# Comparing the tiles of a block with one another for eight pairs of blocks at a time

## The chip, the cores and the metric

The kernel runs on one core of a Trainium2 chip. The metric is the device time of one execution in microseconds (us), and a kernel's time is the median of its runs. The engines are named as in the profile: PE (matrix multiplications), PEld (its weight loads), DVE (vector), ACT (activations), POOL (GpSimd) and SP (which issues DMAs here).

## What is computed

The reference is one residual layer of a graph network, with 12,500 nodes of 64 numbers and 212,500 edges, sorted by `dst`:

```python
def _L0_gnn_ref(h, row, col, dist, eW1, eb1, eW2, eb2, nW1, nb1, nW2, nb2):
    edge_in = jnp.concatenate([h[row], h[col], dist], axis=1)
    e = jax.nn.silu(edge_in @ eW1 + eb1)
    e = jax.nn.silu(e @ eW2 + eb2)
    agg = jax.ops.segment_sum(e, row, num_segments=h.shape[0])
    node_in = jnp.concatenate([h, agg], axis=1)
    out = jax.nn.silu(node_in @ nW1 + nb1) @ nW2 + nb2
    return out
h = jnp.maximum(_layernorm(x, axis=-1), 0.0)
x = x + _L0_gnn_ref(h, src, dst, edge_weight1, ...)
```

The sum runs over `row`, which is `src`: the edges come in the order of the other end, so they have to be brought together by `src` first.

## The kernel before

The nodes are dealt into NB = 100 buckets of 125 by their number modulo 100, and an edge belongs to the bucket of its `src`. The kernel is a counting sort through HBM, followed by dense work on each bucket.

*Blocks and pairs.* The edges are taken in 208 blocks of 1024 (`BLK`), and a block is TB = 8 tiles of 128 edges, one edge on each partition. Two blocks are a pair, and there are NP = 104 pairs. Three tiles in SBUF hold, for every edge, its bucket (`bkE`), its node in the bucket (`locE`) and the first row of its bucket in the HBM table `q` (`offE`). Each is [128 partitions, 16 tiles of a pair, 104 pairs], so the pair is the innermost index, and two tiles of one pair lie 104 numbers (416 bytes) apart. `sources` and `scale` fill them: for pairs 0 to 3 (FIRST = 4) first, and for pairs 4 to 103 in one go later.

*Counting a block: `count(s)`, on DVE and PE.* It is a generator in three parts.
- First part: `oh` (L354) compares the buckets of the block's 8 tiles with the 100 bucket numbers, `each` (L362) sums that over the tiles, and `pick` (L364, or L366 for a whole pair) makes the one-hot columns for the gather of target rows.
- Second part: two small matmuls (L371, L389) carry the running counts `full` in PSUM over from block to block and over the 128 partitions. Then, for the first block of a pair, four DVE instructions (L396 to L402) work for both blocks of the pair. They find, for each edge, how many of the earlier tiles of its block have an edge of the same bucket on the same partition, and add that to `offE`: `eq` compares the 8 tiles with one another, is multiplied by `early` (1 for an earlier tile, times G = 4), is summed into `pre`, and `pre` is added to `offE`.
- Third part: `mine` (L404) and `rank` (L406) read the running count of each edge's bucket, and `to` (L408) adds it to `offE`. That is the edge's row in `q`. `to` has four buffers.

*Sending a block: `send(s)`.* PE gathers the target side of each edge (L429), ACT copies it to `qs` (L439) with the node's number behind it (L445), and POOL writes each tile of 128 edges to the rows `to` of `q` by an indirect DMA (L452): eight to a block, 1661 in all. `qs` has eight buffers of four tiles each. `send(s)` and `count(s + 1)` go hand in hand, part by part.

*The groups.* As ranks fill up, level by level (`LEVELS`), the rows of a bucket are loaded back from `q`, four buckets at a time, and the 450 steps of edge work run over them: `s_lr`, `s_one_t` (`oneT`, L533), `s_pt` (L542, L548), `s_one` (`one`, L561), `s_p2` (L580), `s_seg` (L594), `s_add` (L603, L605). At the end the node network runs bucket group by bucket group (`nodes`).

*The order.* PE, DVE, ACT and SP follow the order in which the program is written. In the first 150 us or so the parts of `send` and `count` alternate with the preparation of the node tables (`norm`, `products` and so on, through `feed`). Later they stand between the steps of the groups, at places that `marks` computes from the levels. POOL has little besides its indirect DMAs. `cnt` is a pool with one buffer for each name, `wk` one with two.

Of the kernel before, what the change touches and what calls it, by code (L numbers as in the profile page):

```python
# [28 lines left out]
F32 = mybir.dt.float32  # L29
# [4 lines left out]
OP = mybir.AluOpType  # L34
AX = mybir.AxisListType
# [3 lines left out]
P = 128  # L39
# [9 lines left out]
TB = BLK // P  # L49
# [12 lines left out]
FIRST = 4  # L62
# [11 lines left out]
def tile_gnn(ctx: ExitStack, tc: tile.TileContext, x, src, dst, ew, eW1, eb1, eW2, eb2, nW1, nb1, nW2, nb2, out):  # L74
    nc = tc.nc
# [6 lines left out]
    NP = -(-E // PAIR)  # L82
# [101 lines left out]
    early = const.tile([P, TB, TB], F32, name="early")  # L184
# [25 lines left out]
    bkE = const.tile([P, 2 * TB, NP], F32, name="bkE")  # L210
    locE = const.tile([P, 2 * TB, NP], F32, name="locE")
    offE = const.tile([P, 2 * TB, NP], F32, name="offE")
# [52 lines left out]
    wk = ctx.enter_context(tc.tile_pool(name="wk", bufs=2))  # L265
    cnt = ctx.enter_context(tc.tile_pool(name="cnt", bufs=1))
    qsp = ctx.enter_context(tc.tile_pool(name="qs", bufs=8))
    top = ctx.enter_context(tc.tile_pool(name="to", bufs=4))
    with ExitStack() as work:
# [59 lines left out]
        def weights(s):  # L329

            if s < nblocks:
                p, g = s // 2, s % 2
                pick = lists[p][1][:, g]
                e0 = s * BLK
                m = 1 if p == 0 or e0 + 2 * BLK > E else 2
                if m == 2 or e0 + BLK <= E:
                    of = bass.AP(tensor=ew.tensor, offset=ew.offset + e0, ap=[[QR, NQR], [BLK, m], [1, QR]])
                    nc.sync.dma_start(lists[p][1][WL::32, g : g + m, :], of)
                else:
                    for a in range(NQR):  # L340
                        m = min(QR, E - e0 - a * QR)
                        if m > 0:
                            of = bass.AP(tensor=ew.tensor, offset=ew.offset + e0 + a * QR, ap=[[m, 1], [1, m]])
                            nc.sync.dma_start(pick[a * 32 + WL : a * 32 + WL + 1, :m], of)

        def count(s):

            if s < nblocks:
                bc, win, pick = blk[s]
                p, g = s // 2, s % 2  # L350
                whole = p > 0 and (2 * p + 2) * BLK <= E
                buckets = bkE[:, g * TB : (g + 1) * TB, p]
                oh = wk.tile([P, TB, NB], BF16, name="oh")
                nc.vector.tensor_tensor(  # L354
                    oh,
                    numbers[:, None, :].to_broadcast([P, TB, NB]),
                    buckets[:, :, None].to_broadcast([P, TB, NB]),
                    op=OP.is_equal,
                )
                each = wk.tile([P, NB], BF16, name="each")  # L360
                with nc.allow_low_precision("whole numbers up to eight"):
                    nc.vector.tensor_reduce(each, oh.rearrange("p t b -> p b t"), AX.X, OP.add)  # L362
                if not whole:
                    nc.vector.tensor_scalar(pick, bc, same, plus, op0=OP.is_equal, op1=OP.add)  # L364
                elif g == 0:
                    nc.vector.tensor_scalar(lists[p][1], lists[p][0], same, plus, op0=OP.is_equal, op1=OP.add)  # L366
            yield
            if s < nblocks and (g == 0 or not whole):
                weights(s)
            if s > 0:  # L370
                nc.tensor.matmul(full, rest, sums.pop(), start=False, stop=True, skip_group_check=True)  # L371
            limits = [(SURE[w], OP.is_gt) for w in ready_at if s == ready_at[w]]
            closed = s > 0 and (s == nblocks or needed[s] != needed[s - 1])
            if closed:
                limits.append((SURE[needed[s - 1]], OP.is_lt))
            if s == nblocks:
                limits.append((ROWS, OP.is_gt))
            if limits:
                u = wk.tile([P, NB], F32, name="u")
                v = wk.tile([P, 1], F32, name="v")  # L380
            for limit, op in limits:
                nc.vector.tensor_scalar(u, full, float(G * limit - 1), None, op0=op)
                nc.vector.tensor_reduce(v, u, AX.X, OP.max)
                nc.vector.tensor_tensor(bad[:, 1:2], bad[:, 1:2], v, op=OP.add)
            if s == nblocks:
                return
            if closed and LEVELS[needed[s - 1]][2]:
                nc.vector.tensor_scalar(full, full, float(G * ENDS[needed[s - 1]] - 1), None, op0=OP.max)
            nc.tensor.matmul(full, before, each, start=False, stop=True, skip_group_check=True)  # L389
            sums.append(each)  # L390
            if g == 0:
                assert p in scaled
                both = bkE[:, :, p].rearrange("p (g t) -> p g t", g=2)
                wide = [P, 2, TB, TB]
                eq = wk.tile(wide, F32, name="eq")
                nc.vector.tensor_tensor(  # L396
                    eq, both[:, :, :, None].to_broadcast(wide), both[:, :, None, :].to_broadcast(wide), op=OP.is_equal
                )
                nc.vector.tensor_tensor(eq, eq, early[:, None].to_broadcast(wide), op=OP.mult)
                pre = wk.tile([P, 2 * TB], F32, name="pre")  # L400
                nc.vector.tensor_reduce(pre.rearrange("p (g t) -> p g t", g=2), eq, AX.X, OP.add)
                nc.vector.tensor_tensor(offE[:, :, p], offE[:, :, p], pre, op=OP.add)  # L402
            yield
            nc.vector.tensor_tensor(mine, oh, full[:, None, :].to_broadcast([P, TB, NB]), op=OP.mult)  # L404
            rank = wk.tile([P, TB], F32, name="rank")
            nc.vector.tensor_reduce(rank, mine, AX.X, OP.add)  # L406
            to = top.tile([P, TB], I32, name="to")
            nc.vector.scalar_tensor_tensor(  # L408
                to, rank, float(G * ROWS - 1), offE[:, g * TB : (g + 1) * TB, p], op0=OP.min, op1=OP.add
            )  # L410
            blk[s].append(to)
            yield
# [60 lines left out]
        def send_all(s0, s1):  # L473

            for s in range(s0, s1):
                load(s + 2)
                i, rest = divmod(s - FILL0, FILL_EACH)
                if rest == 0 and 0 <= i < len(fills):
                    fill(*fills[i])

                for j, _ in enumerate(itertools.zip_longest(send(s), count(s + 1))):
                    pending[needed[s]] -= j == PIECES - 1
                    yield
# [319 lines left out]
        done_a, done_b, ready, scaled = [], [], set(), set()  # L803
# [9 lines left out]
        with tc.tile_pool(name="lists", bufs=1, side="right") as lp:  # L813
# [40 lines left out]
            list(scale(0, FIRST))  # L854
            load(0)
            counting = count(0)
            next(counting)
            todo = groups()
# [47 lines left out]
        for k in range(first, len(steps) + 2):  # L906
            for s in turn:
# [17 lines left out]
                else:  # L925
                    f, ahead = s
# [146 lines left out]
```

## Time and profile before

| | us |
|---|---|
| median of 3 runs | 2463.26 (2462.79 to 2467.51) |
| the profiled execution | 2461.7 |
| its span, first to last instruction | 2459.9 |
| busy: PE | 2045.2 (83%) |
| busy: DVE | 1936.9 (79%) |
| busy: POOL | 1705.5 (69%) |
| busy: ACT | 1088.8 (44%) |
| DVE's four instructions L396 to L402 | 121.7 |

Times in the profile are us from the start of the span. "Busy" is time in which an engine executes an instruction. A wait is put down to whatever released it last. The page has the busy shares in 40 slices of the span, the chain of work that ended last (followed back from the last instruction) and the groups of instructions by cost. The timeline lists single instructions with start and length, and in brackets how long the engine had been idle and what ended that.

### The profile page before, as it was taken

To read this page: it belongs to the slowest core of one execution; us is meant where nothing else is said; L and a number is where in the kernel's file an instruction comes from. 1 tells how busy PE (TensorE), PEld (TensorE's weight loads), DVE (VectorE), ACT (ScalarE), POOL (GpSimd) and SP (SyncE) were. 2 spreads that over 40 slices of the span, in tenths; PEclk is the share of its full clock that TensorE was granted. 3 is DMA by queue.
4 is the path that set the end of the run, shared out by engine and by line. 5 is a ranking of instruction groups with operands and counts; after the bars stand their busy time and mean duration, and the time that the engine had idled before them with its cause. 6 is when DMAs were issued, how large, how long until landed. Compare 5 with 4: busy or idle time off the path is not lost.

```text
span 2459.9 us, 46292 instructions
## 1 busy us (share of the span) xinstructions
PE 2045.2 (83%) x16191; PEld 1829.8 (74%) x16191; DVE 1936.9 (79%) x3006; ACT 1088.8 (44%) x2403; POOL 1705.5 (69%) x1712
## 2 busy tenths in 40 slices
PE   3673776665688898898998988899999999999997
PEld 2452665555587787787887877888888898999986
DVE  7895777676787898787888788898889899886432
ACT  2452333222344454454544444454555555554442
POOL 4777777777777777777777777777777777762110
PEclk9575898877899999999999998999999999999999
DMA  4563566555666765667654544455555556665652
GB/s 116 185 217 124 168 186 193 183 175 171 210 212 211 219 210 180 215 215 227 194 166 165 166 156 161 154 182 165 177 172 181 179 166 207 215 199 174 193 162 67
DMA packets 237006, 443.85 MB, mean 180 GB/s; under 512 B 49804, under 2 KB 108735, under 8 KB 236561
## 3 DMA queue, kind: packets, MB, share of 16 engines
q1 hardware_dynamic: 158629, 269.79, 35.9%
q0 software_dynamic: 53536, 123.03, 14.3%
q10 hardware_dynamic: 24602, 47.98, 6.7%
q8 instruction: 132, 2.16, 0.4%
q14 instruction: 107, 0.88, 0.1%
HBM read 251.07 MB, written 189.55 MB: 179 GB/s over the span
## 4 chain that ended last, share of the span: by engine, by line
PE 36%; DMA 17%; DVE 16%; POOL 13%; issue 8%; ACT 2%; DVEq 0%; POOLq 0%; ACTq 0%; SPq 0%
DMA q<-qs,to 16%; POOL q L452 13%; PE seg L594 8%; PE pt L548 8%; PE p L580 7%; PE pt L542 4%; PE qp L429 4%; DVE oh L354 2%; DVE each L362 2%; DVE oneT L533 2%; PE lr L528 2%; DVE aggT L605 2%; DVE one L561 2%; DVE mine L404 1%; DVE rank L406 1%
## 5 line engine op out<-in xcount | busy, mean ns | idle before, releaser
L452 POOL DMA_INDIRECT q<-qs,to x1661 | 1676.4, 1009 | 586.3 <-issue 396.9
L552 ACT ACTIVATE e<-pt 128x512 f32<-128x512 f32 x450 | 268.7, 597 | 849.8 <-PE pt L548 839.2
L594 PE MATMUL seg<-one,e 128*128 128x125 f32 x3600 | 504.0, 285 | 110.2 <-DVE aggT L605 77.7
L594 PEld LDWEIGHTS seg<-one,e 128*128 128x128 f32 x3600 | 456.0, 199 | 140.0 <-issue 84.7
L580 PEld LDWEIGHTS p<-w,e 128*128 128x128 f32 x3600 | 472.3, 197 | 37.4 <-issue 17.8
L548 PE MATMUL pt<-oneT,a 125*128 125x128 f32 (+1 forms) x2400 | 487.1, 338 | 15.3 <-DVE oneT L533 15.3
L580 PE MATMUL p<-w,e 128*128 128x128 f32 x3600 | 494.1, 281 | 0.0
L548 PEld LDWEIGHTS pt<-oneT,a 125*128 125x128 f32 x2400 | 366.9, 200 | 35.4 <-DVE oneT L533 18.2
L439 ACT COPY qs<-qp 128x512 f32<-128x512 f32 x416 | 224.9, 588 | 356.8 <-PE qp L429 310.1
L533 DVE TENSOR_SCALAR oneT<-lr,part 125x512 f32<-125x512 f32 x450 | 335.0, 745 | 43.4 <-PE lr L528 42.8
L362 DVE TENSOR_REDUCE each<-oh 128x100 bf16<-128x800 bf16 x208 | 315.9, 1519 | 7.2
L561 DVE TENSOR_TENSOR one<-nodes,qt 128x500 f32<-128x500 f32 x450 | 302.4, 672 | 0.2 <-issue 0.2
L542 PE MATMUL pt<-ident,qt 128*128 128x128 f32 x1800 | 287.6, 285 | 1.3 <-DVE oneT L533 1.3
L429 PE MATMUL qp<-win,pick 64*128 64x256 f32 x1662 | 266.3, 435 | 24.2 <-DMA pick<-in_edge_weight_dram 9.1
L584 ACT ACTIVATE e<-p 128x512 f32<-128x512 f32 x450 | 268.7, 597 | 28.7 <-PE p L580 28.7
L574 ACT COPY p<-b2f 128x512 f32<-128x512 f32 x450 | 267.2, 594 | 0.0
L605 DVE TENSOR_TENSOR aggT<-aggT,seg 128x500 f32<-128x500 f32 x275 | 184.0, 669 | 65.5 <-PE seg L594 62.7
L408 DVE SCALAR_TENSOR_TENSOR to<-rank,offE 128x8 int32<-128x8 f32 x208 | 36.2, 174 | 251.3 <-DMA q<-qs,to 246.5
L429 PEld LDWEIGHTS qp<-win,pick 64*128 64x128 f32 x1662 | 162.5, 203 | 81.1 <-issue 44.3
L542 PEld LDWEIGHTS pt<-ident,qt 128*128 128x128 f32 x1800 | 200.7, 148 | 21.3 <-issue 13.4
L406 DVE TENSOR_REDUCE rank<-mine 128x8 f32<-128x800 f32 x208 | 205.1, 986 | 7.2
L404 DVE TENSOR_TENSOR mine<-oh,counts 128x800 f32<-128x800 bf16 x208 | 203.9, 980 | 8.3 <-PE counts L389 8.0
(145 smaller groups left out, 1454.3 us busy)
## 6 DMA issues: line engine op xcount, KB each, us to landing
qt<-q SPq DMA_DIRECT2D x150, 576.0 KB
a<-ta SPq DMA_DIRECT2D x300, 256.0 KB
qt<-q SPq DMA_DIRECT2D x150, 288.0 KB
q<-zeros ACTq DMA_DIRECT2D x25, 1080.0 KB
q<-qs,to POOLq DMA_INDIRECT x1661
q<-zeros ACTq DMA_DIRECT2D x10, 1440.0 KB
bc<-dests SPq DMA_DIRECT2D x103, 128.0 KB
win<-tb SPq DMA_DIRECT2D x416, 30.0 KB
```

Source lines behind the costliest of these rows:

```text
L362: nc.vector.tensor_reduce(each, oh.rearrange("p t b -> p b t"), AX.X, OP.add)
L429: nc.tensor.matmul(qps[i][:, t, : n_of[t]], pick[at, t * P : (t + 1) * P], win[at, : n_of[t]], start=True, stop=True)
L452: ins = nc.gpsimd.indirect_dma_start(out=q[:], out_offset=bass.IndirectOffsetOnAxis(ap=to[:k, j : j + 1], axis=0), in_=qs[:k, t, a, :], in ...
L533: nc.vector.tensor_scalar(oneT, st[k].pop("lr")[:L], part1[:L, :], None, op0=OP.is_equal)
L542: nc.tensor.matmul(pt[:, t, :], qt[:, j, :H], ident, is_transpose=True, start=t == 0, stop=False, skip_group_check=True)
L548: nc.tensor.matmul(pt[:, cols, :], a[:L, b, :], oneT[:, cols, :], start=False, stop=True, skip_group_check=True)
L552: nc.scalar.activation(e1, pt, AF.Silu)
L561: nc.vector.tensor_tensor(one.rearrange("p (b j) l -> p b j l", j=n), nodes1[:, None, None, :].to_broadcast(wide), loc[:, tiles[0][1] : ti ...
L574: nc.scalar.copy(p2, b2f)
L580: nc.tensor.matmul(p2[:, t, :], e1[:, t, :], w2, start=False, stop=t == G - 1, skip_group_check=True)
L584: nc.scalar.activation(e2, p2, AF.Silu)
L594: nc.tensor.matmul(item[2][:, b, :], e2[:, t, :], one[:, t, :], start=j < G, stop=j >= G * (n - 1))
```

## The change

In place of four DVE instructions for each pair, a new function `earlier(g, p0, p1)` does the same for one of the two blocks (`g`) of the pairs `p0` to `p1`, with the pair innermost in `eq` and `pre`. It is called for one pair at a time for pairs 0 to 3, and for eight at a time (EACH) after that: at pair 2 for the first blocks of pairs 4 to 11, at pair 3 for their second blocks, at pairs 10 and 11 for pairs 12 to 19, and so on. The last calls, at pairs 98 and 99, are for the four pairs 100 to 103. So there are 8 calls of one pair, 24 of eight and 2 of four, with four instructions each. `eq` moves from the pool `wk` to `cnt`. The instructions of the other engines and their order stay.

```diff
+        EACH = 8
+
+        def earlier(g, p0, p1):
+
+            if p0 >= p1:
+                return
+            n = p1 - p0
+            wide = [P, TB, TB, n]
+            of = bkE[:, g * TB : (g + 1) * TB, p0:p1]
+            eq = cnt.tile([P, TB, TB, EACH], F32, name="eq")[:, :, :, :n]
+            nc.vector.tensor_tensor(
+                eq, of[:, :, None, :].to_broadcast(wide), of[:, None, :, :].to_broadcast(wide), op=OP.is_equal
+            )
+            nc.vector.tensor_tensor(eq, eq, early[:, :, :, None].to_broadcast(wide), op=OP.mult)
+            pre = wk.tile([P, TB, EACH], F32, name="pre")[:, :, :n]
+            nc.vector.tensor_reduce(pre, eq.rearrange("p t u n -> p t n u"), AX.X, OP.add)
+            off = offE[:, g * TB : (g + 1) * TB, p0:p1]
+            nc.vector.tensor_tensor(off, off, pre, op=OP.add)
+
         def count(s):
...
             if g == 0:
                 assert p in scaled
-                both = bkE[:, :, p].rearrange("p (g t) -> p g t", g=2)
-                wide = [P, 2, TB, TB]
-                eq = wk.tile(wide, F32, name="eq")
-                nc.vector.tensor_tensor(
-                    eq, both[:, :, :, None].to_broadcast(wide), both[:, :, None, :].to_broadcast(wide), op=OP.is_equal
-                )
-                nc.vector.tensor_tensor(eq, eq, early[:, None].to_broadcast(wide), op=OP.mult)
-                pre = wk.tile([P, 2 * TB], F32, name="pre")
-                nc.vector.tensor_reduce(pre.rearrange("p (g t) -> p g t", g=2), eq, AX.X, OP.add)
-                nc.vector.tensor_tensor(offE[:, :, p], offE[:, :, p], pre, op=OP.add)
+                if p < FIRST:
+                    earlier(0, p, p + 1)
+                    earlier(1, p, p + 1)
+                ahead = (p - FIRST) % EACH - (EACH - 2)
+                if ahead >= 0:
+                    p0 = p + 2 - ahead
+                    assert all(i in scaled for i in range(p0, min(p0 + EACH, NP)))
+                    earlier(ahead, p0, min(p0 + EACH, NP))
```

## The prediction

> **What bounds the kernel now.** I read the groups by cost first, then one line over stages, then the chain and the waits, then the timeline.
>
> The first view, the page's costliest groups, gives the scatter on POOL (L452: one indirect DMA per 128 edges) and DVE's last step ahead of it (L408, which writes the offsets `to`). The columns are busy us and mean ns, then idle us before it and what ended most of it. The second view is L452 alone in stages: length, busy us, count.
>
> ```profile
> L452 POOL DMA_INDIRECT q<-qs,to x1661 | 1676.4, 1009 | 586.3 <-issue 396.9
> L408 DVE SCALAR_TENSOR_TENSOR to<-rank,offE 128x8 int32<-128x8 f32 x208 | 36.2, 174 | 251.3 <-DMA q<-qs,to 246.5
> 200.00:2065.00 1865.00, 1430.19 (x1424) 0.93 0.58 183
> ```
>
> 1430.19/1424 is 1.004 us of work for each scatter; the timeline shows 0.30 to 0.31 us between two. 1424 x (1.004 + 0.305) = 1864 us of a stage of 1865 us: from 200 to 2065 us POOL is full. DVE is 79% busy over the span, but it waits 246.5 us at L408 for scatters to finish, because `to` has four buffers. So DVE is ahead, and POOL sets the pace. The chain's last link of that kind over 3 us is at 2068 us:
>
> ```profile
> 1926.08 4.21 DMA q<-qs,to
> 2068.53 3.17 DMA q<-qs,to
> ```
>
> After it PE is the bound (97 to 98% busy from 2100 to 2300 us), and POOL waits for the last blocks.
>
> What lengthens a scatter? The median is 967 ns, the mean 1009: 1661 x 0.042 = 70 us in all. The timeline shows whom it meets (start us, length us):
>
> ```profile
> 1385.95 0.67 DVE L561 TENSOR_TENSOR one<-nodes,qt 128x500 f32<-128x500 f32 x1
> 1386.04 1.42 POOL L452 DMA_INDIRECT q<-qs,to  x1 [0.30 <-issue]
> 1000.88 0.39 DVE L396 TENSOR_TENSOR eq<-bkE 128x128 f32<-128x128 f32 x1
> 1001.07 1.06 POOL L452 DMA_INDIRECT q<-qs,to  x1 [0.31 <-issue]
> 1018.07 1.50 DVE L362 TENSOR_REDUCE each<-oh 128x100 bf16<-128x800 bf16 x1
> 1018.28 0.96 POOL L452 DMA_INDIRECT q<-qs,to  x1 [0.30 <-issue]
> ```
>
> A scatter that starts inside a tensor_tensor with both inputs in SBUF ends 0.84 us after it (1386.62 to 1387.46). The reduce does nothing to it. So an instruction of length T costs POOL (T - 0.15)^2 / (2 x 1.27) us on average: the scatter must start in its first T - 0.15 us, out of a period of 1.27. For L561 that is 0.106 us, x450 = 48 us of the 70.
>
> **The change, part by part.** Prices of the four steps come from the groups with shapes kept apart:
>
> ```profile
> L396 DVE TENSOR_TENSOR eq<-bkE 128x128 f32<-128x128 f32 x104 | 41.6, 400 | 0.0
> L399 DVE TENSOR_TENSOR eq<-eq,early 128x128 f32<-128x128 f32 x104 | 30.4, 292 | 3.6
> L401 DVE TENSOR_REDUCE pre<-eq 128x16 f32<-128x128 f32 x104 | 29.8, 286 | 3.5
> L402 DVE TENSOR_TENSOR offE<-offE,pre 128x16 f32<-128x16 f32 x104 | 19.9, 191 | 3.6
> L406 DVE TENSOR_REDUCE rank<-mine 128x8 f32<-128x800 f32 x208 | 205.1, 986 | 7.2
> L362 DVE TENSOR_REDUCE each<-oh 128x100 bf16<-128x800 bf16 x208 | 315.9, 1519 | 7.2
> L754 DVE SCALAR_TENSOR_TENSOR bkE<-locE,srcE 128x64 f32<-128x64 f32 x1 | 0.2, 224 | 0.0
> ```
>
> *Removed:* 104 x 1.169 = 121.7 us of DVE.
> *Added:* a base of 0.157 us and 1.04 ns an element fit L399, L406 and L754. L396 reads every element 416 bytes apart and pays 1.90 ns; L362 reads 200 bytes apart and pays 1.70. With pairs innermost, eight lie together: I price comparison and product of 512 elements as L754, which has four together (0.157 + 0.533 = 0.690 us each; other end 1.13 at L396's rate). The reduce steps 32 bytes: L362's rate, 1.03 us (ends 0.69 and 1.13). The addition of 64: 0.224. A full call is 2.63 us, and there are 24; two calls of four pairs at 1.63; eight calls of one pair (64 elements) at about 0.97. That is 63.2 + 3.3 + 7.8 = 74 us, so DVE is relieved of 47 us. From 200 to 2065 us this is worth nothing in itself: the cover is the wait at L408, which should grow by about that. Instructions and waits of the other engines, DMAs included, keep their order in the built program. A burst of 2.6 us in place of 1.2, in two of eight pairs, stands ahead of `mine`, `rank` and `to` on DVE; PE and ACT wait for those behind it, and POOL has 17 to 28 us of ready `qs` in that stage. If that cover were gone, each burst would cost 1.4 us.
>
> *The start.* There the cover is thin, and pairs 0 to 3 still run alone, each as two calls, while pairs 2 and 3 run a full call as well. Pitches: two single calls take 1.93 us on DVE where the old group took 1.18, so +0.75; with a full call (2.65) 4.58, so +3.4.
>
> ```profile
> 79.61 0.40 DVE L396 TENSOR_TENSOR eq<-bkE 128x128 f32<-128x128 f32 x1
> 80.98 0.95 DVE L631 TENSOR_REDUCE var<-xs 128x12 f32<-128x768 f32 x1
> 90.19 0.26 ACT L445 COPY qs<-locE 128x64 f32<-128x64 f32 x1
> 93.05 0.97 POOL L452 DMA_INDIRECT q<-qs,to  x1 [0.30 <-ACT rows_a L207]
> 110.65 0.25 ACT L445 COPY qs<-locE 128x64 f32<-128x64 f32 x1
> 114.38 0.96 POOL L452 DMA_INDIRECT q<-qs,to  x1 [0.31 <-issue]
> ```
>
> DVE works without a break to 80 us, and POOL idles 6 us before 82.88, so pair 0's 0.75 shifts everything; pair 1's is swallowed by the 1.03 us that L404 waited at 46.82 for PE. Pair 2's stands ahead of `var` at 80.98, for which ACT waits, with PE's transposes and block 4's `qs` behind it: 79.61 + 4.58 is 84.2, 3.2 later, of which 0.1 was slack. Pair 3's adds 3.4, so DVE is 0.75 + 3.1 + 3.4 = 7.25 us late when block 6's `qs` is made. That `qs` was ready at 110.90, and POOL took it at 114.38, 3.48 later; 0.28 is the least lag seen. So POOL slips by 7.25 - 3.20 = 4.0 us, and, being full afterwards, never makes it up. At contiguous rates throughout it is 2.8, at L396's rate for all 6.5.
>
> *POOL's lengthening.* Before: 49 of the 104 `eq` follow L561 directly in the timeline, overlapping by 0.09 us, so the two act as one hold of 0.98 us: 49 x (0.271 - 0.106) = 8.1, the other 55 x 0.025 = 1.4, the products 0.8; 10.3 us. After: 10 of 24 full calls follow L561: hold 1.27, 10 x (0.494 - 0.106) = 3.9; 14 x 0.115 = 1.6; the products, 24 x 0.115 = 2.8; 8.3 us. So -2.0. The ends: -10.3 if long instructions met no scatter, +6.3 with `eq` at 1.13 us. Chance of the phases alone, over 450 L561 with a spread of 0.16 us each, is +-3.4 us.
>
> The Trainium skill (SBUF — State Buffer, "Who interferes with whom") speaks both ways here. It says the shared port is held for a whole instruction, which is against fewer, longer ones; but it infers that tensor_tensor does not stall descriptor generation, and the 1.06 and 1.42 us scatters above say it does. By that inference this part would be 0 and the sum +3.5.
>
> *The tail.* Past 2065 us DVE loses some 5 groups, with PE at 97%: PE waited 1.2 us there for DVE's L605, so -0.5.
>
> **Sum:** 4.0 - 2.0 - 0.5 = +1.5 on the profiled execution's 2461.7 us (span 2459.9 and 1.8 around it), 2463.2. It lies 1.6 below the median of the runs, 2463.26; on that median the forecast is 2465 us: no change that can be told, 0.2% or 4.9 us being about what a measurement can.
>
> **Rivals.**
> *DVE is the bound after all, and its 47 us come off.* For: 79% busy, 16% of the chain. Against: the 246.5 us of L408, and POOL full to 1 us in 1865. All of it gives 2416; by DVE's share of the chain, 0.16 x 47 = 7.5, it is 2456. 0.10, nearly all near the second.
> *The port is held longer.* On DVE's comparison, in 24 places: from about 0.9 us an `eq` (in place of 0.69) the scatters' lengthening is 11.8, +1.5 on before, and with the start's 4.0 and tail it passes 4.9; at 1.13 us the sum is 6.3 + 4.0 - 0.5, 2473. For: L396's own slow rate. Against: L754. 0.20.
> *The start costs more.* If single calls and full calls run at L396's rate, 6.5 - 2.0 - 0.5 gives 2467; unfavourable phases carry it past 4.9. 0.18.
> *The fused calls don't relieve DVE* (the reduce is as slow as what it replaces): the time stays in the forecast's range, since DVE has room, and its chance is in the forecast's.
>
> **How the numbers follow.** The forecast has 0.50; 0.38 goes to slower (0.20 and 0.18) and 0.12 to faster (DVE's 0.10 and 0.02 of lucky phases). The range of 2457 to 2474 takes the start's 2.8 to 6.5, phases of +-4.4 (1.28 x 3.4), the slow `eq`, and DVE's share nearly to its end; the forecast's own is 2459 to 2468.
>
> **What would show it.** DVE's four lines sum to about 74 us in place of 122; the full `eq` at 0.69 and the full reduce at 1.03; the wait at L408 near 290 us; the mean scatter within 5 ns of 1009; POOL's 49th scatter about 4 us later than 114.38, and full from then to 2065. I am wrong if POOL shows gaps in the middle, if the mean scatter moves by 5 ns or more, or if L408's wait shrinks.

## The result, and the profile after

| | before | after |
|---|---|---|
| median, us | 2463.07 (18 runs, 2459.42 to 2469.38) | 2469.08 (18 runs, 2462.81 to 2474.86) |
| ratio to before | | 1.002, interval 1.001 to 1.0029 |
| the profiled execution, us | 2461.7 | 2474.24 |

The changed kernel is about 6 us slower. The profiled execution of it is among the slowest of its 18, so the 12.5 us between the two profiles are not the size of the change; the profile is read for places.

The costliest groups of the changed kernel (busy us, mean ns, idle us before, what ended most of it), and its scatter in the stage from 200 to 2065 us:

```profile
L469 POOL DMA_INDIRECT q<-qs,to x1661 | 1680.5, 1012 | 595.3 <-issue 397.9
L425 DVE SCALAR_TENSOR_TENSOR to<-rank,offE 128x8 int32<-128x8 f32 x208 | 36.1, 173 | 278.1 <-DMA q<-qs,to 274.1
200.00:2065.00 1865.00, 1429.12 (x1417) 0.93 0.58 183
```

The scatter is L469 now and the step that writes the offsets L425. POOL is nearly as full as before: 1417 x (1.0085 + 0.305) is 1861 of 1865 us. DVE waits 274.1 us for scatters in place of 246.5. That is 28 of the 46 us that it was relieved of; its waits for PE grew as well (75.4 us for 62.7 ahead of `aggT`, 54.7 for 42.8 ahead of `oneT`).

DVE's groups of the changed kernel, with shapes kept apart: comparison, product, sum and addition in the calls of eight pairs, then two of them in the calls of one.

```profile
L356 DVE TENSOR_TENSOR eq<-bkE 128x512 f32<-128x512 f32 x24 | 16.4, 684 | 0.0
L359 DVE TENSOR_TENSOR eq<-eq,early 128x512 f32<-128x512 f32 x24 | 16.6, 693 | 0.8
L361 DVE TENSOR_REDUCE pre<-eq 128x64 f32<-128x512 f32 x24 | 26.0, 1082 | 0.8
L363 DVE TENSOR_TENSOR offE<-offE,pre 128x64 f32<-128x64 f32 x24 | 5.6, 233 | 0.8
L356 DVE TENSOR_TENSOR eq<-bkE 128x64 f32<-128x64 f32 x8 | 2.2, 276 | 0.0
L361 DVE TENSOR_REDUCE pre<-eq 128x8 f32<-128x64 f32 x8 | 2.2, 269 | 0.3
```

The prices are those foreseen. A full call is 2.69 us, and all calls together are 76 us in place of 122. So the 6 us were not lost on DVE's own account.

The timeline shows where POOL falls behind: at the start. In the changed kernel, ACT's copies that complete the first `qs` of blocks 4 and 6, and POOL's 33rd and 49th scatters, which take them up:

```profile
95.41 0.26 ACT L462 COPY qs<-locE 128x64 f32<-128x64 f32 x1
95.94 0.97 POOL L469 DMA_INDIRECT q<-qs,to  x1 [1.76 <-ACT hr L664]
119.40 0.25 ACT L462 COPY qs<-locE 128x64 f32<-128x64 f32 x1
119.92 0.96 POOL L469 DMA_INDIRECT q<-qs,to  x1 [3.27 <-ACT qs L462]
```

Before, these two scatters started at 93.05 and 114.38 us without a wait. Now POOL waits 1.76 and 3.27 us for rows to send, and its 49th scatter is 5.5 us late. From there POOL is nearly full in both kernels. Up to the 1501st scatter it stands still for 5.4 us beyond the 0.304 us between two scatters, before for 2.2; most of that is four gaps of 0.58 to 2.21 us, where before had one of 1.16 us. The longest:

```profile
884.71 1.28 POOL L469 DMA_INDIRECT q<-qs,to  x1 [2.21 <-issue]
```

At the 1501st scatter the changed kernel's profile is 13.8 us behind (2030.2 and 2016.4): 5.5 us from the start, 3.2 from these gaps, and 5.1 from scatters that lasted longer.

### The profile page after: what moved, and what is told of

Same layout as the page of the kernel before. It is cut to its first block, busy times and chain, and to the rows that moved or that the text cites. A ratio compares the mean times of both kernels' runs of the same rounds, so it can differ in the third digit from the quotient of the medians.

```text
span 2472.5 us, 46004 instructions
## 1 busy us (share of the span) xinstructions
PE 2050.6 (83%) x16191; PEld 1834.2 (74%) x16191; DVE 1899.8 (77%) x2726; ACT 1088.4 (44%) x2403; POOL 1709.5 (69%) x1712
## 4 chain that ended last, share of the span: by engine, by line
PE 39%; DMA 18%; DVE 14%; POOL 13%; issue 8%; ACT 2%; DVEq 0%; POOLq 0%; ACTq 0%; SPq 0%
DMA q<-qs,to 17%; POOL q L469 13%; PE seg L611 9%; PE pt L565 8%; PE p L597 8%; PE pt L559 4%; PE qp L446 4%; PE lr L545 2%; DVE oneT L550 2%; DVE oh L373 2%; DVE each L381 2%; DVE one L578 2%; DVE aggT L622 1%; DVE mine L421 1%; DVE rank L423 1%
## 5 line engine op out<-in xcount | busy, mean ns | idle before, releaser
L469 POOL DMA_INDIRECT q<-qs,to x1661 | 1680.5, 1012 | 595.3 <-issue 397.9
L550 DVE TENSOR_SCALAR oneT<-lr,part 125x512 f32<-125x512 f32 x450 | 335.0, 744 | 55.1 <-PE lr L545 54.7
L425 DVE SCALAR_TENSOR_TENSOR to<-rank,offE 128x8 int32<-128x8 f32 x208 | 36.1, 173 | 278.1 <-DMA q<-qs,to 274.1
L622 DVE TENSOR_TENSOR aggT<-aggT,seg 128x500 f32<-128x500 f32 x275 | 184.0, 669 | 77.1 <-PE seg L611 75.4
L446 PEld LDWEIGHTS qp<-win,pick 64*128 64x128 f32 x1662 | 164.0, 205 | 83.2 <-issue 41.9
```

What stands on the lines that cost most here:

```text
L446: nc.tensor.matmul(qps[i][:, t, : n_of[t]], pick[at, t * P : (t + 1) * P], win[at, : n_of[t]], start=True, stop=True)
L469: ins = nc.gpsimd.indirect_dma_start(out=q[:], out_offset=bass.IndirectOffsetOnAxis(ap=to[:k, j : j + 1], axis=0), in_=qs[:k, t, a, :], in ...
L550: nc.vector.tensor_scalar(oneT, st[k].pop("lr")[:L], part1[:L, :], None, op0=OP.is_equal)
```

## The experiments

The theory of the start says that the loss is made in the first 120 us, where POOL has under 4 us of ready rows, and is never made up. The rivals: longer comparisons hold POOL's scatters up (the port), and DVE's relief is worth something in the middle. All ratios are to the kernel before, run beside them.

**One half, then the other.** The calls of eight begin with pair 12, and pairs 0 to 11 keep the old group:

```diff
+                if p < FIRST + EACH:
+                    both = bkE[:, :, p].rearrange("p (g t) -> p g t", g=2)
...
-                if p < FIRST:
-                    earlier(0, p, p + 1)
-                    earlier(1, p, p + 1)
                 ahead = (p - FIRST) % EACH - (EACH - 2)
-                if ahead >= 0:
+                if p >= FIRST and ahead >= 0:
```

> Pairs 0 to 11 keep the old group of four instructions for each pair; calls of eight pairs begin with pairs 12 to 19. So the first 130 us are those of before, and the middle is that of the changed kernel. Theory of the start (the loss is made where POOL has under 4 us of ready rows): the 49th scatter starts at 114.4 us as before, and the time is before's within 2 us, 2461 to 2465. Rival, the port (long comparisons hold POOL's scatters up): the loss stays, +4 to +7, with a mean scatter over 1.012 us. Rival, DVE's relief is worth something in the middle: under 2460.

Measured: 2464.51 us (12 runs), ratio 1.001, interval 0.9999 to 1.002. POOL's 49th scatter, and all its scatters:

```profile
114.41 0.97 POOL L477 DMA_INDIRECT q<-qs,to  x1 [0.30 <-issue]
L477 POOL DMA_INDIRECT q<-qs,to x1661 | 1683.7, 1014 | 588.6 <-issue 393.0
```

The start is that of before, and most of the loss is gone. DVE's relief in the middle brought nothing. Whether 2 us of loss or none are left, this run does not say. The mean scatter is 1.014 us, over the 1.012 that the port rival named, but the loss that it named is not there; further down this length turns out to be that of `one`, not of the comparisons.

The other half: single calls for pairs 0 to 3 and one call for each half of pairs 4 to 11, then the old group.

```diff
                 if p < FIRST:
                     earlier(0, p, p + 1)
                     earlier(1, p, p + 1)
+                if p >= FIRST + EACH:
+                    both = bkE[:, :, p].rearrange("p (g t) -> p g t", g=2)
...
-                if ahead >= 0:
+                if p < FIRST and ahead >= 0:
```

> The other half: single calls for pairs 0 to 3 and one call of eight for each half of pairs 4 to 11, then the old group for each pair from 12 on. Theory of the start: the whole loss is here, 49th scatter near 119.9 us, time +4.5 to +6.5 on before. The port: 49th scatter as late, but made up or not seen at the end, time within 2 us of before.

Measured: 2468.28 us (12 runs), ratio 1.0027, interval 1.0016 to 1.0038.

```profile
119.60 0.97 POOL L480 DMA_INDIRECT q<-qs,to  x1 [3.27 <-ACT qs L473]
```

The whole loss is here, in twelve pairs of 104, with the same wait of 3.27 us. The theory of the start holds.

**A smaller burden on the start.** The changed kernel, but with the old group for pairs 0 to 3:

```diff
                 if p < FIRST:
-                    earlier(0, p, p + 1)
-                    earlier(1, p, p + 1)
+                    both = bkE[:, :, p].rearrange("p (g t) -> p g t", g=2)
...
```

> As the changed kernel, but pairs 0 to 3 keep the old group, so only the calls of eight at pairs 2 and 3 burden the start. Theory of the start, by its own sum: DVE is 2.7 us late after pair 2 and 5.4 after pair 3, less 3.2 us of lead, so the 49th scatter is 2.1 us later than before, about 116.5 us, and the time is +2 (0 to 4). If the loss is the port's: the same +6 as the changed kernel.

Measured: 2465.45 us (12 runs), ratio 1.0015, interval 1.0003 to 1.0026.

```profile
116.15 0.97 POOL L477 DMA_INDIRECT q<-qs,to  x1 [0.91 <-ACT qs L470]
```

The sum said 116.5; block 6's `qs` was 5.0 us late in place of 5.4. So the rule "lateness less 3.2 us of lead" gives the size too, and the medians go with the 49th scatter: 1.8 us late here and +3.2 us at the end, 5.2 to 5.5 late and about +6 in the two kernels with the full burden. By the time alone the rival's +6 is not excluded here: the interval goes from 0.7 to 6.4 us.

**The port by itself.** The kernel before, but the row of node numbers that L561 compares with is read from PSUM:

```diff
-        counts = sgp.tile([P, 2 * NB], F32, name="counts")
-        full, numbers = counts[:, :NB], counts[:, NB:]
+        counts = sgp.tile([P, 2 * NB + L], F32, name="counts")
+        full, numbers, nodesP = counts[:, :NB], counts[:, NB : 2 * NB], counts[:, 2 * NB :]
...
+        nc.vector.tensor_copy(nodesP, nodes1)
...
-                nodes1[:, None, None, :].to_broadcast(wide),
+                nodesP[:, None, None, :].to_broadcast(wide),
```

> The kernel before, with one edit: the comparison that makes the one-hot `one` (L561) reads its row of node numbers from PSUM, so that only one of its inputs is in SBUF. Theory (POOL is the bound from 200 to 2065 us and two SBUF inputs hold its scatters up): L561 keeps its 0.67 us, the mean scatter falls from 1.009 to about 0.98 us, and the time falls by 30 to 48 us, less where PE takes over as the bound. Rival (DVE or PE is the bound): the scatters get shorter or not, the time stays within 3 us of before.

Measured: 2423.15 us (5 runs), ratio 0.984, interval 0.9824 to 0.9856. Its groups, and its scatter from 200 to 2065 us:

```profile
L453 POOL DMA_INDIRECT q<-qs,to x1661 | 1623.3, 977 | 601.1 <-issue 385.8
L562 DVE TENSOR_TENSOR one<-counts,qt 128x500 f32<-128x500 f32 x450 | 300.8, 668 | 6.2 <-PE counts L390 5.5
200.00:2065.00 1865.00, 1419.05 (x1459) 0.94 0.58 188
```

The comparison takes 0.668 us as before (0.672), but the mean scatter falls from 1.009 to 0.977 us, 1661 x 0.032 = 53 us, and 39 us of them arrive at the end. POOL is still full (1459 x 1.278 = 1864 us), with 35 more scatters in the same stage. That shows both halves of the reading of the profile: POOL is the bound, and a DVE instruction with two SBUF inputs lengthens its scatters.

**How much the joined comparisons change at the port.** In each profile a scatter over 0.972 us can be given to the DVE instruction that ends 0.84 us before it. That was done for the comparisons, products and additions (less what L561 alone would have cost) and for `one`:

```
                          comparisons and products    one
before                            8.3 us            46.7 us
after                             7.4               55.6
calls of eight from pair 12       7.5               58.2
old group for pairs 0 to 3        7.3               47.0
```

The change at the port is 0 to -1 us. The part of `one`, an instruction that the change does not touch, moves by 11 us between executions, as its 450 instances meet the scatters differently. That fits the spread of the runs: 29 of the kernel before, run beside the experiments so far, lie between 2456 and 2469 us, the five with `one` off the port between 2421.4 and 2425.2. Five are few, and that the phases cause this spread was not tried apart.

**A dose of DVE work, with and without the port.** The kernel before, with one more instruction of 128 x 800 in each group from pair 12 on: first a product of two SBUF inputs, then a reduce with one. (Two arrays for it are filled once, at the very start.)

```diff
+                if p >= FIRST + 8:
+                    nc.vector.tensor_tensor(junk2, junk, junk, op=OP.mult)
```

```diff
+                if p >= FIRST + 8:
+                    nc.vector.tensor_reduce(junk2[:, :, 0], junk, AX.X, OP.add)
```

> The kernel before, with one more DVE instruction in each group from pair 12 on (92 of them): a product of two SBUF inputs, 128 x 800, about 0.99 us, whose result nobody reads. Theory (POOL is the bound; DVE has room; two SBUF inputs hold a scatter up): (0.99 - 0.15)^2 / (2 x 1.27) = 0.28 us each, +26 us in all (20 to 33), mean scatter near 1.024 us. Rival (DVE is the bound): 92 x 0.99 = +91 us. Rival (neither): within 4 us of before.

> The same place and length, 92 times 0.99 us, but a reduce with one SBUF input. Theory: it holds no scatter up, so the time is before's within 4 us, the mean scatter stays at 1.01 us, and the wait for the offsets' buffers on DVE shrinks by up to 90 us. Rival (DVE is the bound): +91 us.

The kernel before itself took 3110 us on the chip that these ran on. Measured: ratios 0.9991 (0.9968 to 1.0013) for the product and 1.0015 (0.9994 to 1.0036) for the reduce. Their scatters, the product's first:

```profile
L458 POOL DMA_INDIRECT q<-qs,to x1661 | 1674.7, 1008 | 1250.4 <-ACT qs L451 740.9
L458 POOL DMA_INDIRECT q<-qs,to x1661 | 1653.2, 995 | 1243.2 <-ACT qs L451 734.4
```

Both were run again, with the same expectations:

> The extra reduce of 0.99 us in 92 groups once more, on a chip where the kernel before takes 2463 us. Theory (POOL is the bound, DVE has room, a reduce holds no scatter up): within 4 us of before, mean scatter 1.01 us, and DVE's wait for the offsets' buffers down from 246 us to about 160. Rival (DVE is the bound): +91 us.

> The extra product of two SBUF inputs of 0.99 us in 92 groups once more. Theory: +26 us (20 to 33), mean scatter near 1.024 us. Rival (DVE is the bound): the same +91 us as with the reduce. Rival (neither): within 4 us.

Measured: 0.9992 (0.996 to 1.0023) for the reduce and 0.9998 (0.9967 to 1.0029) for the product, with the kernel before at 3056 us. Groups and longest wait with the reduce, then the group with the product:

```profile
L458 POOL DMA_INDIRECT q<-qs,to x1661 | 1654.5, 996 | 1228.8 <-ACT qs L451 713.1
POOL q L458 <- ACT qs L451: 713.1, 164, 22.5
```

```profile
L458 POOL DMA_INDIRECT q<-qs,to x1661 | 1690.0, 1017 | 1150.2 <-ACT qs L451 647.9
```

In all four executions POOL waits 650 to 740 us for rows, and single engines wait up to 19 us at a time for something that the profile does not name (all five at once for 4.8 us at most). So POOL is not full, and neither dose can reach the end: the +26 us were not tested. DVE's wait at the offsets, foreseen at about 160 us, is gone altogether. What can be read is the port. The product makes the scatters 21.5 us longer in all than the reduce of the same length does on the first chip (1674.7 less 1653.2) and 35.5 on the second (1690.0 less 1654.5), where 26 were foreseen. Given to the instructions as above, without the chance part of `one`, the product's own share is 25.9 and 31.2 us, and no scatter falls to the reduce. (The means stay under those foreseen, because `one` costs only 29 to 32 us where POOL has gaps.)

**The versions that follow from it.** Calls of eight from pair 12 on with the node numbers in PSUM, and the same with the mask and a copy of the eight pairs' buckets in PSUM too, so that comparison and product have one SBUF input each:

```diff
...
+            cp = copyP[:, :, :n]
+            nc.vector.tensor_copy(cp, of)
             nc.vector.tensor_tensor(
-                eq, of[:, :, None, :].to_broadcast(wide), of[:, None, :, :].to_broadcast(wide), op=OP.is_equal
+                eq, of[:, :, None, :].to_broadcast(wide), cp[:, None, :, :].to_broadcast(wide), op=OP.is_equal
             )
-            nc.vector.tensor_tensor(eq, eq, early[:, :, :, None].to_broadcast(wide), op=OP.mult)
+            nc.vector.tensor_tensor(eq, eq, earlyP[:, :, :, None].to_broadcast(wide), op=OP.mult)
```

> The row of node numbers in PSUM (as in the run that gained 39 us) together with calls of eight pairs from pair 12 on. Theory: with the start left alone and POOL still the bound, joining the pairs is worth nothing here: within 3 us of 2423. Rival (DVE's relief counts once POOL is faster): under 2420.

> As the one before, and the joined comparison and product also read one input each from PSUM (the mask, and a copy of the eight pairs' buckets that costs one more small DVE copy in each call). Theory: the comparisons then hold up no scatter of POOL; they cost 3.6 us in the profiled execution with the node numbers in PSUM, so 2418 to 2423, 2 to 4 us under the kernel without it.

On the chip where the kernel before took 3110 us they were at 1.0141 (1.0117 to 1.0166) and 1.014 (1.0115 to 1.0166): slower there, for reasons that stay open. Run again where it took 2465.53:

> Node numbers in PSUM and calls of eight from pair 12 on, with the comparisons' inputs in SBUF, once more. Theory (POOL stays the bound, DVE's relief is worth nothing): 0.983 to 0.985 of the kernel before. Rival (DVE's relief counts once POOL is faster): under 0.982.

> Node numbers, mask and a copy of the eight pairs' buckets in PSUM, calls of eight from pair 12 on, once more; where the kernel before takes 2463 us. Theory (the comparisons then hold up no scatter, and the start is that of before): 0.981 to 0.983 of the kernel before, against 0.984 for the node numbers in PSUM alone; mean scatter 0.975 us or less. Rival (PE or DVE has become the bound): 0.984 or more with the scatters as short.

Measured: the first 2424.85 us, ratio 0.9831 (0.9818 to 0.9845); the second 2422.05 us, 0.9825 (0.9812 to 0.9839). The second's scatter:

```profile
L482 POOL DMA_INDIRECT q<-qs,to x1661 | 1615.3, 972 | 609.1 <-issue 400.5
200.00:2065.00 1865.00, 1415.58 (x1463) 0.94 0.59 188
```

In the second, 97% of the scatters take less than 0.975 us now, against 83% before. The two kernels are 41 and 43 us faster than the kernel before. Against the node numbers in PSUM alone (0.984, run on another chip) neither is apart: the ratios differ by 2 and 4 us, less than their intervals.

## Why the prediction was right or wrong

The time, 2469.08 us, lies in the range of 2457 to 2474, and 1 us outside the forecast's own 2459 to 2468. The forecast was no change that can be told, with 4.9 us as the line. Measured are +6.0 us, with an interval of 2.5 to 7.1 that has the line in it: the runs do not decide between the forecast and a small loss that can just be told. The sum said +1.5; with its terms as measured, 5.5 for the start and at most -1 at the port, it is +4.5 to +5.5 without the tail.

*POOL is the bound, DVE's relief goes into waiting.* Right in the main. The wait grew from 246.5 to 274.1 us (290 foreseen), and the calls of eight from pair 12 on gained nothing. But one of the signs of being wrong, gaps of POOL in the middle, showed in small: 3.2 us more than before in the one profile. The prediction held POOL covered there by 17 to 28 us of ready `qs` and gave this no term. Over the executions where POOL is full, such gaps up to the 1501st scatter come to 2.1 to 5.4 us in the five with calls of eight in the middle and to 1.9 to 2.6 in the three without: 0 to 3 us that may be theirs, not told from chance.

*The prices on DVE.* Right: the comparison 0.684 us for 0.690, the reduce 1.082 for 1.03, single calls 0.995 for 0.97, 76 us in all for 74.

*The start, +4.0 us.* The mechanism was right, with its 3.2 us of lead, and so was pair 1's share of nothing (DVE's wait for PE there, the one longer break before 80 us, shrank from 1.03 to 0.28 us); the size was off. `qs` of block 6 was 8.75 us late in place of 7.25, and 8.75 - 3.2 is the 5.5 measured. Three pieces make the difference. Pair 0 shifted the first scatter by 1.2 us for 0.75: two single calls took 2.03 us, and 0.35 had gone before they began, which is chance between two executions. Pairs 2 and 3 added 3.4 and 3.5 for 3.1 and 3.4. And PE, which was taken as unchanged, lost 0.9 us; some 0.3 of all that met slack. PE's part is in the timelines: the same products, before at 83.03 and after at 87.31 us, then in the kernel with the node numbers in PSUM, whose start is that of before; each with the stage around it (PE, PEld, DVE, ACT and POOL busy, then the granted PE clock):

```profile
83.03 1.30 PE L204 MATMUL ab<-w,hr 64*128 64x128 f32 x16 [1.32 <-ACT hr L647]
81.00:84.70 3.70, 2.11 (x20) 1.56 (x20) 3.03 (x5) 3.05 (x12) 1.52 (x2) 0.92 0.37 126
```

```profile
87.31 2.24 PE L204 MATMUL ab<-w,hr 64*128 64x128 f32 x16 [4.12 <-ACT hr L664]
84.70:90.00 5.30, 2.69 (x18) 2.24 (x18) 4.88 (x8) 1.84 (x7) 4.08 (x5) 0.50 0.25 80
```

```profile
83.20 2.24 PE L204 MATMUL ab<-w,hr 64*128 64x128 f32 x16 [1.08 <-ACT hr L648]
81.00:84.70 3.70, 2.19 (x15) 1.79 (x17) 2.92 (x6) 2.54 (x10) 1.35 (x2) 0.50 0.36 122
```

In the profile before, the sixteen products fell into a few microseconds at a granted clock of 0.92 and took 1.30 us; in the changed kernel they met 0.50 and took 2.24. The shift is not shown to be the reason: with the start of before, at 82.8 to 83.2 us, they took 2.24, 2.24, 2.19 and 1.55 us in four more executions. So this piece is luck of the one profile that the sum was read from. Part of the 3.2 us of lead is luck too: block 6's `qs` waited 3.48 us for POOL in that profile and 2.21 in the third execution shown here. Its 49th scatter still started at 114.22 us, so the loss of 5.5 us does not depend on this.

*POOL's lengthening, -2.0 us.* 0 to -1 in the profiles, and never seen in a time: the calls of eight from pair 12 on came out at +2.3 us with an interval that ends at nothing. (The 0.15 us in its formula is 0.13 by its own rows, 0.967 less 0.84. With that, `one` is priced at 53 us in place of 48; it cost 46.7 to 58.2.) The mean scatter rose by 2.5 ns, inside the 5 that were allowed. It was not worth a term of its own beside the +-3.4 us of `one`.

*The tail, -0.5 us.* Too small to be told apart.

*The rivals.* DVE as the bound fell with the calls of eight from pair 12 on, which relieve DVE and gain nothing. The port held longer fell with the other half, where the comparisons of the middle are the old ones and the whole loss is there; `eq` took 0.684 us, far from the 0.9 where it would decide, and the table gives the comparisons no more than before. The start that costs more is what happened, in size, but not for the reason given, since the instructions ran at the rates of the forecast.

Where the Trainium skill (SBUF — State Buffer, "Who interferes with whom") infers that tensor_tensor does not stall descriptor generation, the run with the node numbers in PSUM decides against it for this indirect DMA: 0.032 us on the mean scatter and 39 us of time. Which part of the scatter is held up, no run here shows. The same section's rule, that an instruction with at most one SBUF input, outside the modes that use two ports, does not contend with GpSimd, is what that run used, and its mean scatter agrees. One SBUF input alone is no safeguard: before, a scatter beside two TENSOR_SCALAR of 128x1600 with one SBUF input (51.38 and 52.40 us) took 2.03 us.

## What to carry to other kernels

Work saved on an engine that is ahead was worth nothing here, and batching it ahead of time cost where the pipeline had no lead yet: look up the least lead in the first blocks, and add up what is moved ahead of it. Where POOL's indirect DMAs are the bound, look at their durations rather than at their count alone, and at which DVE instructions they overlap: moving one small operand to PSUM was worth 39 us where POOL is the bound, six times what the change cost. On a chip where the kernel before took 3110 us and POOL was not full, the two kernels with that move were 1.4% slower, so look first whether POOL is full. A term of 2 us cannot be forecast where chance meetings of two engines are worth 46.7 us in one execution and 58.2 in another. And one profile does not give the price of a chain of a few microseconds on PE: look at the same place in several.

## What was not expected of the hardware

The granted clock of PE from 81 to 84.7 us was 0.92, 0.90, 0.78, 0.72 and 0.50 in five executions with the same start, and sixteen equal products there took between 1.30 and 2.24 us; nothing in the instruction counts shows it. Reading one input of a comparison from PSUM cost DVE nothing (0.668 us for 0.672). And the same kernel took 2462 to 2466 us on some chips and 3056 and 3110 on two others, where single engines waited at times for something that the profile does not name.
